# Macaron layer on one Trainium2 core: two first-key steps instead of one beside each unit of the last down-projection

## The chip, the cores and the metric

The kernel runs on one core of one Trainium2 chip. The metric is the device time of one execution in microseconds (us). All data are 32-bit floats. The engines are PE (matrix multiplication), DVE (vector), ACT (scalar functions), POOL (general) and SP, whose queue here issues most of the transfers.

## What is computed

The input x has 4 batches of 512 rows and 512 columns. The layer is a feed-forward part, an attention part and the same feed-forward part again:

```
x = x + 0.5 * ffn(layernorm(x))
x = x + attention(layernorm(x))
x = x + 0.5 * ffn(layernorm(x))

ffn(h):       gate, up, down = weights interpolated from a few control points (Catmull-Rom spline)
              return (silu(h @ gate.T) * (h @ up.T)) @ down.T          # 512 -> 2048 -> 512
attention(h): q, k, v, z from h @ W_qkvz; beta, g from h @ W_ba
              q, k, v = silu(conv of 4 taps along the rows)             # 16 key heads, 32 value heads
              q, k = rms_norm(q), rms_norm(k), each used by 2 value heads
              for each row t: S = S * exp(g_t)
                              S = S + k_t (x) ((v_t - k_t S) * beta_t)  # delta rule
                              o_t = q_t S
              return (rms_norm(o) * norm_w * silu(z)) @ W_out
```

## The kernel before

The first feed-forward part (`ffn`) goes batch by batch. A turn for batch b+1 computes gate and up products on PE, silu on ACT and the product of both on DVE, and stores the hidden values to memory; POOL then gathers them back in the order in which the spline's structure repeats (`gather`). The down-projection of a batch (`project`, a nested function of `ffn`) has 32 "units": 4 `sums` (the pm matmuls, line 482), 16 `blocks` (y, L492, 3 or 4 groups of 32 rows in 4 PSUM banks), 4 `rest` (L495) and 8 `total` (L498). ACT then moves each of the four y tiles to yg, and four more units, `back(g)`, transpose yg into y_pt (L509, in the PSUM banks of y) and add y_pt to the residual ffn_xr piece by piece on DVE (L537). After the last of them SP stores the batch (L515). The four `back` units of a batch are run at the start of the next turn, or, for the last batch, at the very end (`plan["tail"]`).

The attention works through 64 pairs of batch and key head, in "slots". Ahead of slot 0 stand its first steps, a generator (`attention`) that the feed-forward part drives through the argument `beside`: each `next` emits one step. There are 90: 13 for the layernorm of batch 0 and its transposition, then 77 for the first eight keys, seven for each key number `un`, overlapped over three key numbers. In the first four steps of a key one matmul of its projection pj is emitted (L1041; w_k is its weight, loaded by L1091). A step or more later follow the four taps of the convolution (ACT acc L1049, three DVE acc L1051), the silu (ACT th L1059, DVE k L1063), and with the seventh step two keys later the key's small blocks (PE pkk L1072, ACT ksq L1112, mean square on DVE L1077 to L1080, POOL rsk L1082, weights L1124 to L1130, POOL wed L1134, the scan L1141 and dd L1144). With the seventh step of key 2 come the gate sums `sums` (pgs L1012, pe L1021), whose result goes through memory: decay_c and decay_b (L1027, with a POOL memset L1025 ahead of each) and back as ad (L1103). Each step also lets the inverse of the first four keys' triangular blocks (`invert`, DVE L1155 to L1174) advance twice, once it has been made, which is with the seventh step of key 6. The last three DVE instructions of the first steps are memsets of tt and nn (L1695), and the generator then yields None. Slot 0 begins with pj of w_q and w_v and the block pqq (L1072, of q).

During these first steps PSUM has one bank for all products of the attention (pj, pgs, pe), since the four y banks and the two of pm hold the rest, and w_k has one buffer. The order on PE, DVE, ACT and POOL is the order in which the program emits (`by_hand`); each engine executes in that order. A scheduler orders SP in this part. `later(n, f)` puts f into a calendar that `tick` works off, n ticks on; the first steps have a calendar of their own with their own ticks. In `run`, each round emits one gather step, one unit and one first step.

The last part of `ffn` in the kernel before is then: a run over the 16 units left from batch 2 with a first step each; the four `back` units of batch 2 with a first step each; 14 first steps alone; 32 units of batch 3 with a first step each; the four `back` units of batch 3 with a first step each; then the 20 first steps that are left.

Of the kernel before, what the change touches and what calls it, by code (L numbers as in the profile page):

```python
# [23 lines left out]
NT = S // P  # L24
# [240 lines left out]
def tile_macaron(ctx, tc, x, w_qkvz, w_ba, conv_w, dt_bias, a_log, norm_w, w_out, cps, consts, grid, starts, out):  # L265
    nc = tc.nc
    B = x.shape[0]
# [31 lines left out]
    def ffn(src, dst, build, beside=iter(())):  # L299
        with ExitStack() as st:  # L300
# [21 lines left out]
            def tick():  # L322
                clock[0] += 1
                for f in calendar.pop(clock[0], ()):
                    f()

            def drain():
                while calendar:
                    tick()

            def load(b, name, pool):
                xt = pool.tile([P, NT, H], F32, name=name)
                nc.sync.dma_start(xt, src(b).rearrange("(t p) h -> p t h", p=P))
                return xt
# [14 lines left out]
            def features(xt):  # L349

                xnT = io.tile([P, NC, S], F32, name="ffn_xnT")
                ft = [fp.tile([P, S], F32, name="ft") for _ in range(NG_F)]
                xn, stat = {}, {}

                def stats():
                    stat["mv"], stat["rstd"] = statistics(xt)

                def norm(t):
                    mv, rstd = stat["mv"], stat["rstd"]
                    xn[t] = wk.tile([P, H], F32, name="ln_xn", bufs=3)  # L360
                    nc.vector.tensor_scalar(
                        xn[t], xt[:, t, :], mv[:, t, 0:1], rstd[:, t : t + 1], ALU.subtract, ALU.mult
                    )

                def turn(t):
                    pt = ps.tile([P, NC, P], F32, name="ln_pt", tag="tp")
                    for c in range(NC):
                        nc.tensor.transpose(pt[:, c, :], xn[t][:, c * P : (c + 1) * P], ident)
                    later(1, lambda: nc.scalar.copy(xnT[:, :, t * P : (t + 1) * P], pt))

                def interpolate(g):
                    pf = ps.tile([P, S], F32, name="pf", tag="tp")
                    for c in range(NC):
                        nc.tensor.matmul(
                            pf[NODES * c : NODES * (c + 1)], lag[:, c, NODES * g : NODES * (g + 1)], xnT[:, c, :],
                            start=True, stop=True,
                        )
                    later(1, lambda: nc.scalar.copy(ft[g], pf))

                turns = [lambda t=t: turn(t) for t in range(NT)]  # L380
                inter = [lambda g=g: interpolate(g) for g in range(NG_F)]
                return ft, stats, [lambda t=t: norm(t) for t in range(NT)], turns, inter
# [44 lines left out]
            def hidden(b, ft):  # L427

                to, box = hid[b % 2], {}

                def gate(k):
                    if build and b == 0:
                        block(k, wr, we, cm)
                    product(k, 0)

                def product(k, m):
                    at = (k % 2) * P
                    pm = box[m] = gu.tile([P, S], F32, name=("pg", "pu")[m], tag="gu")
                    nc.tensor.matmul(pm, wc[k // 2][:, m, at : at + P], ft[k // 2], start=True, stop=True)  # L439
                    if m:  # L440
                        pg = box[0]
                        later(1, lambda: finish(k, pg, pm))

                def finish(k, pg, pu):
                    sg = wk.tile([P, S], F32, name="ffn_sg")
                    nc.scalar.activation(sg, pg, AF.Silu)
                    it = wk.tile([P, S], F32, name="ffn_it", bufs=4)
                    nc.vector.tensor_tensor(it, pu, sg, ALU.mult)  # L448
                    nc.sync.dma_start(to[k * P : (k + 1) * P, :], it)

                return [f for k in range(NB) for f in (lambda k=k: gate(k), lambda k=k: product(k, 1))]

            def gather(b):
                to, nat = hid[b % 2], []

                def step(v):
                    nt = np_.tile([P, S], F32, name="nat")
                    nc.gpsimd.indirect_dma_start(  # L458
                        out=nt, out_offset=None, in_=to[:, :],
                        in_offset=bass.IndirectOffsetOnAxis(ap=idx[:, v : v + 1], axis=0),  # L460
                    )
                    nat.append(nt)

                return nat, [lambda v=v: step(v) for v in range(NB)]
# [82 lines left out]
            plan = {"nxt": None, "tail": [], "ft": ft}  # L547

            def turn_of(b):


                main = hidden(b + 1, plan["ft"]) if b + 1 < B else []
                norms, turns, inter = [], [], []
                if plan["nxt"]:
                    plan["ft"], _, norms, turns, inter = plan["nxt"]
                    plan["nxt"] = None
                units, back = [], []
                if b >= 0:
                    units, back = project(b, plan["nat"])
                plan["nat"], steps = gather(b + 1)  # L560
                tail, early_ = plan["tail"], []
                for i in range(4):
                    early_ += [*tail[i : i + 1], *turns[i : i + 1]]
                early_ += inter
                lead = 6 * 2 if b >= 0 else len(main)
                for i, f in enumerate(main):
                    if b + 3 < B:
                        if i == 16:
                            xt = load(b + 3, "ffn_x", io)
                        if i == 28:  # L570
                            plan["nxt"] = features(xt)
                            plan["nxt"][1]()
                    for n_ in norms[i : i + 1]:
                        n_()
                    f()
                    tick()
                    n = -(-len(early_) // max(1, lead - i)) if i < lead else 0
                    if i >= 2 or not turns:
                        for f in early_[:n]:
                            f()  # L580
                            tick()
                        early_ = early_[n:]
                    if i >= lead:
                        keep = 16 if b + 2 == B else 0
                        n = -(-(len(units) - keep) // (len(main) - i))
                        for f in units[:n]:
                            f()
                            tick()
                        units = units[n:]
                drain()  # L590
                plan["tail"] = back
                return early_ + units, steps if b + 1 < B else []

            def run(units, steps, beside=iter(())):
                while units or steps:
                    for f in steps[:1]:
                        f()
                    for f in units[:1]:
                        f()
                        tick()  # L600
                    next(beside, None)
                    units, steps = units[1:], steps[1:]

            by_hand = lambda *more: tc.manual_schedule(
# [6 lines left out]
            if build:  # L611
                first = hidden(0, plan["ft"])
                ft, _, norms, turns, inter = plan["nxt"] or (None, None, [], [], [])
# [16 lines left out]
            with by_hand(nc.sync):  # L630
                left = [], []
                if build:
                    plan["nat"], steps = gather(0)
                    left = [], steps
                for b in range(0 if build else -1, B - 1):
                    run(*left)
                    left = turn_of(b)

            early.close()
            with by_hand():  # L640
                also = beside if B > 2 else iter(())
                run(*left, also)
                units, _ = turn_of(B - 1)
                run(units[:NT], [], also)

                for _ in range(14):
                    next(also, None)
                run(units[NT:], [], also)
                run(plan["tail"], [], also)
                drain()  # L650
                for step in beside:
                    if step is None:
                        break

    def spline_weights(st, scratch, wc, ps):

# [1053 lines left out]

    steps = attention()
    ffn(lambda b: x[b], lambda b: x1[b], True, steps)
    for _ in steps:
        pass
    ffn(lambda b: x2[b], lambda b: out[b], False)


# [30 lines left out]
```

## Time and profile before

| what | value |
|---|---|
| time, median of 3 runs | 3822.8 us (3818.41, 3822.8, 3823.15) |
| profiled execution, its own time | 3876.63 us |
| span of the profiled execution | 3874.8 us |
| mean granted PE clock in it | 0.966 |
| PE, DVE, ACT, POOL busy, share of the span | 93%, 68%, 38%, 22% |
| batch 2's last units and batch 0's layernorm, then the 14 steps alone | to 392 us, then to 410 us |
| 32 units of batch 3 and its y_pt | 410 to 467 us |
| rest of the first steps | to 514 us |

The profile is one execution on the chip. Its times are microseconds from the start of the span. A timeline row gives the start, the length, the engine, the line of the kernel, the operation, its output and inputs, the shape, how many instructions are merged and, in brackets, how long the engine was idle before it and which instruction ended the wait. One fp32 product of PE appears as more than one matmul record, so a pj step of one contraction block is a row "x2". A row of the window table gives the busy time of each engine in one stretch, the granted PE clock as a share of full speed, the busy share of the DMA engines and what they moved.

### The profile page before, as it was taken

The numbers are of one execution on the slowest core, as the hardware profiler recorded it, in microseconds if no ns is written. First come the engines' busy times: TensorE is split into PE (matmuls) and PEld (weight loads), VectorE is DVE, ScalarE is ACT, GpSimd is POOL, SyncE is SP. The second block draws the span as 40 slices with busy tenths as digits, with TensorE's granted clock in tenths as the row PEclk, the third lists the DMA queues.
The fourth block names the chain that finished last, engine by engine and source line by source line (L and its number), as shares of the span: only waits on it lengthen the run. The fifth ranks groups of instructions, "written<-read, shape, count | busy, mean of one in ns | idle before, by whom it ended". The sixth has DMA issues, their size and how long they took to land.

```text
span 3874.8 us, 62477 instructions
## 1 busy us (share of the span) xinstructions
PE 3587.5 (93%) x24568; PEld 1969.3 (51%) x24568; DVE 2633.2 (68%) x5928; ACT 1464.5 (38%) x3440; POOL 852.4 (22%) x655
## 2 busy tenths in 40 slices
PE   5988779999999999999999999999999999988798
PEld 2333345555555555555555555555555555553233
DVE  5223687878878788788878887877888777643221
ACT  2322124444444444444444444444444434433121
POOL 2113112222222222222222222222222222211211
PEclk8999889999999999999999999999999999989998
DMA  4435321222222222122112221221222111104442
GB/s 140 150 117 187 88 66 47 62 63 61 59 65 70 80 64 71 51 63 61 58 58 80 66 62 57 64 73 58 60 84 60 54 61 58 55 12 157 148 144 87
DMA packets 303094, 302.25 MB, mean 78 GB/s; under 512 B 96881, under 2 KB 231313, under 8 KB 302225
## 3 DMA queue, kind: packets, MB, share of 16 engines
q1 hardware_dynamic: 292560, 264.70, 22.0%
q0 software_dynamic: 10240, 33.56, 2.8%
q8 instruction: 194, 3.18, 0.3%
q14 instruction: 100, 0.81, 0.1%
HBM read 247.60 MB, written 50.59 MB: 77 GB/s over the span
## 4 chain that ended last, share of the span: by engine, by line
PE 44%; DVE 36%; ACT 8%; POOL 5%; issue 3%; another core or an unknown queue 1%; DMA 1%; SPq 0%; DVEq 0%; ACTq 0%; POOLq 0%
DVE acc L1051 12%; PE py L1507 7%; PE pz L1359 6%; DVE vT L1063 4%; PE pj L1041 4%; PE pg L439 3%; PE pu L439 3%; PE y L492 3%; POOL oo L1480 3%; DVE ee L1227 3%; PE pks L1398 2%; POOL orr L1479 2%; ACT tq L1415 2%; PE pu L1344 2%; ACT oo L1485 2%
## 5 line engine op out<-in xcount | busy, mean ns | idle before, releaser
L1051 DVE SCALAR_TENSOR_TENSOR acc<-pj,cw,acc 128x511 f32<-128x511 f32 (+2 forms) x768 | 573.5, 747 | 160.1 <-ACT acc L1049 141.2
L1041 PE MATMUL pj<-xnT,w_v 128*128 128x512 f32 x1024 | 521.0, 602 | 0.0
L1507 PE MATMUL py<-w_o,gT 128*128 128x512 f32 x1024 | 514.9, 616 | 0.4
L1359 PE MATMUL pz<-w_z,xnT 128*128 128x512 f32 x1024 | 514.5, 614 | 0.0
L448 DVE TENSOR_TENSOR ffn_it<-pu,ffn_sg 128x512 f32<-128x512 f32 x128 | 88.4, 691 | 406.4 <-PE pu L439 231.6
L1041 PE MATMUL pj<-xnT,w_q 128*128 128x512 f32 x512 | 255.9, 603 | 9.4 <-ACT ksq L1112 9.4
L1041 PE MATMUL pj<-xnT,w_k 128*128 128x512 f32 x512 | 254.7, 599 | 3.9 <-DVE acc L1051 3.2
L1415 ACT ACTIVATE tq<-pks,rqe 128x128 f32<-128x128 f32 x384 | 120.4, 364 | 339.7 <-DVE rq L1256 195.9
L1059 ACT ACTIVATE th<-acc 128x512 f32<-128x512 f32 x256 | 163.0, 637 | 216.9 <-DVE acc L1051 215.3
L1485 ACT ACTIVATE oo<-oo,orr 128x128 f32<-128x128 f32 x512 | 162.6, 389 | 205.9 <-POOL oo L1480 205.9
L1049 ACT ACTIVATE acc<-pj,cw 128x512 f32<-128x512 f32 x256 | 175.3, 685 | 160.4 <-PE pj L1041 159.1
L1507 PEld LDWEIGHTS py<-w_o,gT 128*128 128x128 f32 x1024 | 171.6, 192 | 106.4 <-issue 95.3
L1359 PEld LDWEIGHTS pz<-w_z,xnT 128*128 128x128 f32 x1024 | 169.7, 190 | 99.5 <-issue 88.5
L1082 POOL TENSOR_TENSOR rsq<-msq,phalf 128x4 f32<-128x4 f32 x64 | 64.9, 1014 | 681.6 <-DVE msq L1080 681.6
L1082 POOL TENSOR_TENSOR rsk<-msk,phalf 128x4 f32<-128x4 f32 x64 | 66.9, 1045 | 664.5 <-DVE msk L1080 657.4
L1041 PEld LDWEIGHTS pj<-xnT,w_v 128*128 128x128 f32 x1024 | 170.6, 191 | 70.8 <-issue 64.1
L1241 POOL TENSOR_TENSOR ks<-kn,ws 128x1024 f32<-128x1024 f32 x64 | 121.8, 1902 | 378.2 <-DVE ws L1234 358.9
L1063 DVE SCALAR_TENSOR_TENSOR vT<-th,acc 128x512 f32<-128x512 f32 x128 | 184.8, 1444 | 23.1 <-ACT th L1059 23.1
L458 POOL DMA_INDIRECT nat<-hid,idx x128 | 122.9, 960 | 337.0 <-PE y_pt L509 134.2
L1473 DVE TENSOR_REDUCE om<-osq 128x4 f32<-128x512 f32 x128 | 87.1, 681 | 139.6 <-ACT osq L1472 139.6
L1166 DVE TENSOR_TENSOR inv<-inv,inv_tmp 128x30 f32<-128x30 f32 (+14 forms) x480 | 169.0, 352 | 16.5
L1423 PEld LDWEIGHTS pzz<-rr,tt 128*128 128x128 f32 x768 | 114.9, 193 | 113.1 <-issue 54.7
(213 smaller groups left out, 6874.5 us busy)
## 6 DMA issues: line engine op xcount, KB each, us to landing
hid<-ffn_it SPq DMA_DIRECT2D x128, 256.0 KB
w_v<-in_L_attn_W_qkvz SPq DMA_DIRECT2D x64, 512.0 KB
w_z<-in_L_attn_W_qkvz SPq DMA_DIRECT2D x64, 512.0 KB
ab<-decay_c SPq DMA_DIRECT2D x64, 512.0 KB
w_o<-in_L_attn_W_out SPq DMA_DIRECT2D x32, 1024.0 KB
w_k<-in_L_attn_W_qkvz SPq DMA_DIRECT2D x64, 256.0 KB
w_q<-in_L_attn_W_qkvz SPq DMA_DIRECT2D x64, 256.0 KB
ad<-decay_b SPq DMA_DIRECT2D x256, 32.0 KB
```

Of the source, the lines that this page charges most:

```text
L439: nc.tensor.matmul(pm, wc[k // 2][:, m, at : at + P], ft[k // 2], start=True, stop=True)
L1041: nc.tensor.matmul(pj, w()[:, c, col : col + DK], xnT[:, c, :], start=c == 0, stop=c == NC - 1)
L1049: nc.scalar.activation(acc, pj, AF.Copy, scale=cw[:, ch, 3:4])
L1051: nc.vector.scalar_tensor_tensor(acc[:, d:], pj[:, : S - d], cw[:, ch, 3 - d : 4 - d], acc[:, d:], ALU.mult, ALU.add)
L1059: nc.scalar.activation(th, box["acc"], AF.Tanh)
L1063: nc.vector.scalar_tensor_tensor(dest(), box["th"], 1.0, box["acc"], ALU.add, ALU.mult)
L1082: nc.gpsimd.tensor_tensor(rs, ms, phalf[:, :NT], ALU.pow)
L1166: nc.vector.tensor_tensor(ee[:, j + 1 :, :j], ee[:, j + 1 :, :j], tj, ALU.add)
L1359: nc.tensor.matmul(pz, xnT[:, c, t * P : (t + 1) * P], pair["wz"][:, c].rearrange("p j k -> p (j k)"), start=c == 0, stop=c == NC - 1,)
L1415: nc.scalar.activation(tq[:, r], pks[:, 1, r], AF.Copy, scale=s["rqe"][:, t, r : r + 1])
L1485: nc.scalar.activation(s["oo"][:, t, r], s["oo"][:, t, r], AF.Copy, scale=s["orr"][:, u : u + 1])
L1507: nc.tensor.matmul(box["py"], pair["gT"][r][:, t, :], pair["wo"][:, r, :], start=r == 0, stop=r == 3)
```

## The change

`run` gets a number `pace`: how many first steps follow each unit. For the turn of batch 3 (its four `back` units of batch 2 and 32 units of down-projection, in one run now) and for the four `back` units of batch 3 it is two instead of one. The 14 steps alone are dropped. With 16 steps beside batch 2's units, 72 beside the 36 units and two more, all 90 steps are emitted by the first two `back` units of batch 3, so none are left for the end. The generator is wrapped so that it stops at its None; what follows None stays behind the feed-forward part, as before. Each step and unit emits what it emitted before.

```diff
-            def run(units, steps, beside=iter(())):
+            def run(units, steps, beside=iter(()), pace=1):
                 while units or steps:
                     for f in steps[:1]:
                         f()
                     for f in units[:1]:
                         f()
                         tick()
-                    next(beside, None)
+                    for _ in range(pace):
+                        next(beside, None)
                     units, steps = units[1:], steps[1:]
...
             with by_hand():
-                also = beside if B > 2 else iter(())
+                first_steps = iter(beside.__next__, None)
+                also = first_steps if B > 2 else iter(())
                 run(*left, also)
-                units, _ = turn_of(B - 1)
-                run(units[:NT], [], also)
-
-                for _ in range(14):
-                    next(also, None)
-                run(units[NT:], [], also)
-                run(plan["tail"], [], also)
+                run(*turn_of(B - 1), also, 2)
+                run(plan["tail"], [], also, 2)
                 drain()
-                for step in beside:
-                    if step is None:
-                        break
+                for _ in first_steps:
+                    pass
```

On PE the order between pj of key 1 and the first pgs and pm changes, then pj and y alternate in another proportion. On DVE the last additions of ffn_xr (batch 3) come after the work of the last keys, with the memsets among them, instead of in the middle of the inversion. On SP the store of batch 2 is issued earlier, the store of batch 3 later, and the loads of w_k, ad, ab and w_o change their places. On POOL ee (L1221) moves behind one more rsk.

## The prediction

> **What bounds the kernel now.** I read the page first, for who is busy over the whole run, then the table of 10 us windows, to see which engine bounds the stretch that the change touches, then the timelines of PE, DVE and the DMA queue (SP) there.
>
> The page's first part: PE is busy nearly always, so the end moves only by what PE idles.
>
> ```profile
> PE 3587.5 (93%) x24568; PEld 1969.3 (51%) x24568; DVE 2633.2 (68%) x5928; ACT 1464.5 (38%) x3440; POOL 852.4 (22%) x655
> ```
>
> Windows (length, then busy us of PE, PEld, DVE, ACT, POOL, then PE's clock, DMA share, GB/s):
>
> ```profile
> 400.00:410.00 10.00, 5.47 (x18) 2.61 (x18) 5.18 (x12) 2.22 (x5) 0.00 (x0) 0.96 0.09 26
> 430.00:440.00 10.00, 10.00 (x94) 3.48 (x94) 5.09 (x13) 1.48 (x3) 1.93 (x2) 1.00 0.18 41
> 470.00:480.00 10.00, 0.00 (x0) 0.00 (x0) 9.72 (x31) 0.90 (x2) 0.00 (x0) 0.53 0.44 129
> 490.00:500.00 10.00, 3.81 (x5) 1.73 (x6) 9.21 (x31) 0.27 (x1) 1.40 (x2) 0.50 0.20 55
> 530.00:540.00 10.00, 10.00 (x113) 5.15 (x111) 7.33 (x18) 5.14 (x11) 4.08 (x2) 1.00 0.10 29
> ```
>
> Three stages. To 410 PE has holes: the 14 steps alone. From 410 to 467 PE is full and DVE half idle. From 467 to 520 DVE is full and PE stands: DVE sets that end, and whatever PE saves ahead of it counts only if DVE's stretch starts sooner. From 520 on PE is full again, so a shift at 520 reaches the end of the kernel.
>
> PE's timeline (start, length, line, operation, what it waited for):
>
> ```profile
> 392.37 5.21 PE L1041 MATMUL pj<-xnT,w_k 128*128 128x512 f32 x8
> 400.76 3.67 PE L1041 MATMUL pj<-xnT,w_k 128*128 128x512 f32 x8 [3.18 <-DVE acc L1051]
> 407.62 0.68 PE L1012 MATMUL pgs<-g,cst 128*128 128x128 f32 x4 [3.18 <-issue]
> 424.59 1.10 PE L1041 MATMUL pj<-xnT,w_k 128*128 128x512 f32 x2 [0.71 <-ACT fm L484]
> 436.24 1.12 PE L1041 MATMUL pj<-xnT,w_k 128*128 128x512 f32 x2
> 486.10 0.66 PE L1072 MATMUL pkk<-k 128*32 128x32 f32 x32 [19.21 <-DVE k L1063]
> 496.19 6.22 PE L1041 MATMUL pj<-xnT,w_q 128*128 128x512 f32 x8 [9.44 <-ACT ksq L1112]
> 502.25 4.45 PE L1041 MATMUL pj<-xnT,w_v 128*128 128x512 f32 x10
> 519.39 0.66 PE L1072 MATMUL pqq<-q 128*32 128x32 f32 x32 [12.69 <-DVE q L1063]
> 519.98 3.78 PE L1041 MATMUL pj<-xnT,w_v 128*128 128x512 f32 x4
> ```
>
> DVE's timeline: the inversion starts at 458.95, and from there DVE works without a break to the last memset.
>
> ```profile
> 454.94 2.32 DVE L1051 SCALAR_TENSOR_TENSOR acc<-pj,cw,acc 128x511 f32<-128x511 f32 x3 [4.20 <-ACT acc L1049]
> 458.95 1.94 DVE L1155 STREAM_TRANSPOSE inv<-dd 128x1024 f32<-128x1024 f32 x1
> 485.87 1.50 DVE L537 TENSOR_TENSOR ffn_xr<-y_pt,ffn_xr 128x4 f32<-128x4 f32 x16
> 513.52 0.48 DVE L1695 MEMSET nn<- 64x512 f32 x1
> ```
>
> SP's timeline: fourth key's load, and the store of the last batch.
>
> ```profile
> 421.47 0.40 SPq L1091 DMA_DIRECT2D w_k<-in_L_attn_W_qkvz x1
> 487.40 0.36 SPq L515 DMA_DIRECT2D x<-ffn_xr x1
> ```
>
> The load lands in time for the matmul at 424.59, 3.1 us after its issue.
>
> **The change part by part.** No instruction is added or dropped; the order changes between 375 and 525 us. All is set against the profiled execution (3876.63 us, 54 above the median 3822.8; the difference is carried over).
>
> *1. The 14 steps alone go.* They took 392.4 to 410.5, with 6.9 us of PE holes (3.18, 3.18, 0.58). Now they stand between the four transpositions of batch 2 and the first sums and blocks. That hides the holes but delays the chain. Key 1's last matmul comes at 398.2 behind two more y_pt groups, its taps on DVE behind more ffn_xr additions, so key 2 starts at 402.9 (was 400.8). The first y matmuls need the banks of y_pt1 to y_pt3, free after the last ffn_xr of batch 2 at about 406.7, and key 2's last matmul is queued behind them: 411, so pgs at 414.2 (was 407.6). On SP and POOL follow decay_c, the memset, decay_b, eight ad issues (4.71 us) and key 4's w_k: 13.9 us from pgs before, some 0.9 less now, since the store of batch 2 is issued ahead of them. w_k at 427.1, its matmul at 430.2 instead of 424.59: **+5.6**.
>
> *2. Two steps a unit.* A key has 7 steps, four with a matmul of 1.07 us. Before: 7 units of 1.07 and 4 of 1.07 are 11.7 us, the distance of 424.59 and 436.24. Now 3.5 units: 8.1 us of PE work. But next key's first matmul needs the only bank, free 3.05 us after the last matmul (ACT acc 0.69, three DVE acc 2.32), and the only w_k buffer, 3.1 us from issue to use. Before, 4 units (4.3 us) covered that; now two and a pkk cover 2.0, so PE waits 1.1: 9.2 us a key. Two keys and key 6's own matmuls gain 5.3 of the 5.6. The inversion starts at 459.2: **+0.3**. PE's saved holes thus end at a DVE that starts no sooner.
>
> A rule bears on the 3.1 us. The Trainium skill, "DMA: Bandwidth & Descriptors", section "Anatomy of one DMA — SWDGE (gpsimd) path", puts a transfer at 2.0 us and its bytes at 436 GB/s: an estimate of 2.6 for these 256 KB, on a path that isn't this queue. It would make the key 8.7 and the sum 1.3 lower. I take the trace's 3.1.
>
> *3. DVE's stretch.* From 458.95 to 514.00 are 55.05 us. The operations stay, the last additions of ffn_xr (0.84+1.25+1.50+1.66+1.50 = 6.75 us) move to its end. Of the small waits (0.79, 1.19, 0.79 on POOL) the scan ee now covers one: **−0.8**. So it ends at T = 513.5.
>
> *4. What has lost its cover.* In before w_q and five w_v matmuls ran at 496 to 507 in DVE's shadow. Now w_q's first matmul takes the bank of y_pt3, whose last ffn_xr addition is DVE's last work before T. So w_q (6.06 us), ACT's copy (0.69), then taps q to pqq (515.62 to 519.39, 3.77) follow T: pqq at T+10.8 instead of T+5.4: **+5.4**. PE is warm then, so the w_v group behind it, 3.78 at a clock of 0.58 to 0.74, takes 2.0 with what surrounds it: **−1.6**.
>
> A rule speaks here: the skill's "TensorE: Matmul & The Clock Gate", section "What's actually happening", has PE at half clock after an idle window of about 3.4 us, and full after 3.4 us of work. By it w_q would be cold for 3.4 and then twice as fast, 4.8 us, the sum 1.3 lower. The row has clock 0.50 and 6.06 us for all four contraction steps, after holes as long as those expected here: I take 6.06.
>
> *5. Moved at no cost.* SP: the last x store is issued at T, and q's silu and pqq wait for its landing; before it landed after some 5.6 us (as the store at 415.2 did), needed at T+10: 4 us of slack. ab, w_q, w_v, w_z wait for the last FFN matmul (480.3, as it is queued behind key 7's pkk, which waits for DVE's k at 477.5): ab at 487.4, needed at 495.6. w_o moves behind ad: not used for long. POOL: ee stands behind one more rsk (1.0), with the same slack. ACT: yg2 and yg3 behind ksq at 486.5, needed at 503. If such a cover is gone, DVE or pqq waits for the excess, 1:1.
>
> Sum: 0.3 − 0.8 + 5.4 − 1.6 = **+3.3 us**, 0.09%. About 0.2% (7.6 us) is what a measurement of this kernel can tell from no change, so this is no change: 3826, its own range 3821 to 3832, for the front's +5.6 (2 to 8) and w_q's 4.8 to 6.1.
>
> **The rivals.** *Slower: the keys keep no 9.2 us.* Place: 425 to 455, where DVE has its taps in order with the rest. Each key has some 5 us of DVE work (5.09 in an 11.7 us key's window) and ACT's part; if taps find an addition, a th or a mean square ahead of them, bank and next key are late, and y behind the matmul too. Price: 1.5 to 3 us a key, three keys, 4.5 to 9 ahead of the inversion, passed on whole: 3831 to 3835. It decides from 10.6 us a key (3 × 1.4 = 4.3, with 3.3 over 7.6). For: DVE's in-order queue, one bank, one buffer. Against: DVE idles 4.20 ahead of a tap at 454.94. More of the same kind (a front later than 430) reaches 3841.
>
> *Faster: the gain stays.* Keys at 8.1 us (the load hidden) and a front late by 2 instead of 5.6 start the inversion at 452.3, 6.9 sooner; if w_q also isn't held (the bank free before DVE's end), 5.4 less its 1.6 go too, and if DVE's two small waits left on POOL (1.19 and 0.79) are covered as the third is, 2.0 more: 3.3 − 6.9 − 3.8 − 2.0 = −9.4, or 3813. For: 6.9 us of holes do vanish. Against: the 3.18 waits in the trace on exactly this bank; a gain needs two steps wrong together.
>
> *It doesn't do what it says:* the order on all engines does move, so only a shift that cancels is left; it is in the first case.
>
> **How the numbers follow.** Forecast 0.55 (0.40 within 0.2%, 0.15 above by the upper ends of its terms); slower rival 0.29; faster rival 0.16 (0.14 past −0.2%, 0.02 within). Slower 0.44, same 0.42, faster 0.14. Range 3813 to 3839 leaves out some 0.1 below and 0.1 above.
>
> **What would show it.** Right: pgs near 414, key 4 near 430, keys 9.2 apart with holes of 1 us, inversion near 459, w_q after the last ffn_xr near 513.5, pqq near 524. Wrong: inversion before 455 or w_q ahead of DVE's end (faster); keys over 10.6 apart, or pqq waiting for the x store (slower).

## The result: slower by 0.3%, and the profile after

| | kernel before | changed kernel |
|---|---|---|
| time, median of 8 runs | 3824.48 us (3818.41 to 3827.38) | 3835.24 us (3833.35 to 3838.28) |
| ratio to before | | 1.0029, 95% interval 1.0019 to 1.0038 |
| span of the profiled execution | 3874.8 us | 3831.9 us |

The change costs 10.8 us (by the interval 7 to 15). The forecast case, 3826, is 9 us too low, and the time lies above its own range (3821 to 3832); the whole range, 3813 to 3839, holds it by the part given to the slower rival.

The span of before is from an execution that is long elsewhere: from the last output projection of the attention (the last start of py, 3503.0 there and 3492.5 in the changed kernel) to the end it took 372 us, the changed kernel's 339. So the two traces are not laid over each other from the start of the span but from the end of pb, the gate projection ahead of key 1: 391.49 in before (384.82 + 6.67), 372.05 in the changed kernel. pb starts 9.0 us after the first matmul of key 0 in both (375.80 and 357.38), so up to there the change shifted nothing. All times below called "from pb" are so counted. In before pb itself took 1.03 us longer; a second trace of before (e5) bounds what this does to the comparison.

PE's timeline of the changed kernel, from pb to slot 0 (columns as in the prediction):

```profile
366.41 5.64 PE L948 MATMUL pb<-wba,xnT 128*128 128x64 f32 x32 [2.74 <-issue]
383.25 1.10 PE L1037 MATMUL pj<-xnT,w_k 128*128 128x512 f32 x2 [3.43 <-DVE acc L1047]
386.01 2.92 PE L492 MATMUL y<-nat,wr 32*128 32x512 f32 x4 [0.38 <-DVE ffn_xr L537]
388.86 3.46 PE L1037 MATMUL pj<-xnT,w_k 128*128 128x512 f32 x4
397.55 0.68 PE L1008 MATMUL pgs<-g,cst 128*128 128x128 f32 x4 [2.11 <-issue]
414.54 2.04 PE L1037 MATMUL pj<-xnT,w_k 128*128 128x512 f32 x2 [4.73 <-DVE w L1124]
416.51 2.09 PE L492 MATMUL y<-nat,wr 32*128 32x512 f32 x8
426.13 1.96 PE L1037 MATMUL pj<-xnT,w_k 128*128 128x512 f32 x4 [0.65 <-DVE acc L1047]
435.25 1.10 PE L1037 MATMUL pj<-xnT,w_k 128*128 128x512 f32 x2 [1.87 <-DVE dd L1140]
436.28 2.09 PE L492 MATMUL y<-nat,wr 32*128 32x512 f32 x8
446.24 1.96 PE L1037 MATMUL pj<-xnT,w_k 128*128 128x512 f32 x4 [0.65 <-DVE acc L1047]
502.68 6.27 PE L1037 MATMUL pj<-xnT,w_q 128*128 128x512 f32 x8 [23.55 <-issue]
513.58 0.46 PE L1068 MATMUL pqq<-q 128*32 128x32 f32 x32 [0.34 <-DVE q L1059]
513.97 1.98 PE L1037 MATMUL pj<-xnT,w_v 128*128 128x512 f32 x4
```

Keys 4 to 7 start at 414.54, 426.13, 435.25 and 446.24: 11.6, 9.1 and 11.0 us apart, where 9.2 was predicted. The long distances are those that begin with a long hole (4.73 and 1.87 us), and after these holes PE is slow: the same eight y matmuls that take 1.14 us elsewhere take 2.09. The window table says that this is the clock (PEclk, third number from the end):

```profile
380.00:390.00 10.00, 6.38 (x12) 2.21 (x13) 6.47 (x29) 1.59 (x4) 0.00 (x0) 0.75 0.25 90
...
410.00:420.00 10.00, 5.46 (x13) 1.90 (x14) 3.38 (x11) 0.79 (x2) 1.99 (x2) 0.66 0.25 50
420.00:430.00 10.00, 9.35 (x74) 3.06 (x73) 5.10 (x13) 1.58 (x3) 1.31 (x1) 1.00 0.17 39
430.00:440.00 10.00, 8.13 (x64) 3.00 (x63) 5.09 (x13) 1.58 (x3) 2.54 (x3) 0.83 0.18 41
```

Narrower windows of the same table place the changes. The granted clock is 0.50 ("cold" below; "warm" is 1.00) from 385.04 to 391.87, 398.70 to 402.11, 412.35 to 419.18 and 436.24 to 439.66. These stretches are one or two times 3.41 us long, and they start 4, 4 and 7 times 3.41 us apart: the clock changes on a fixed grid, and it does so in all ten traces. In the step of the grid ahead of the last fall, 432.83 to 436.24, PE was busy for 45%, since the hole of 1.87 us lies wholly in it.

The wait of 4.73 us is put down to a DVE operation (w, L1124) that ended at 414.50. That is a coincidence: in e1 below, with the same order on PE and DVE, this matmul starts 3.4 us before that operation. SP's timeline has the true releaser. The load of key 4's weight stands behind eight ad issues, is issued at 411.42, 3.1 us ahead of the matmul, and lands 3.0 us later.

```profile
406.54 4.78 SPq L1099 DMA_DIRECT2D ad<-decay_b  x8
411.42 0.40 SPq L1087 DMA_DIRECT2D w_k<-in_L_attn_W_qkvz  x1
502.61 0.38 SPq L515 DMA_DIRECT2D x<-ffn_xr  x1
```

Key 6's weight, not held up by ad, is issued at 431.10 and lands only after 4.0 us (keys 5 and 7: 2.8), just ahead of the matmul at 435.25. That is the hole of 1.87 us; why this load was slow is open.

DVE's timeline, the inversion's start, the taps of a key, and the two ends of its stretch:

```profile
443.82 2.31 DVE L1047 SCALAR_TENSOR_TENSOR acc<-pj,cw,acc 128x511 f32<-128x511 f32 x3 [5.77 <-ACT acc L1045]
447.83 1.93 DVE L1151 STREAM_TRANSPOSE inv<-dd 128x1024 f32<-128x1024 f32 x1
498.18 4.40 DVE L537 TENSOR_TENSOR ffn_xr<-y_pt,ffn_xr 128x12 f32<-128x12 f32 x35
502.49 1.91 DVE L1151 STREAM_TRANSPOSE inv<-dd 128x1024 f32<-128x1024 f32 x1
```

The inversion starts 75.8 us from pb (before: 67.5), the stretch ends, where the next transposition starts, at 130.4 (122.4), pqq starts at 141.5 (127.9), and the third matmul step of key 8, well inside slot 0, at 148.5 (137.7). These are 8.3, 8.0, 13.6 and 10.9 us more. The last one is the measured cost: from there the shift stays at 9 to 11 us to the end of the attention.

### The profile page after: what moved, and what is told of

Its sections match the earlier page's. It is cut to its first block, busy times and chain, and to the rows that moved or that the text cites. A ratio compares the mean times of both kernels' runs of the same rounds, so it can differ in the third digit from the quotient of the medians.

```text
span 3831.9 us, 62480 instructions
## 1 busy us (share of the span) xinstructions
PE 3582.2 (93%) x24568; PEld 1965.4 (51%) x24568; DVE 2632.5 (69%) x5928; ACT 1463.6 (38%) x3440; POOL 851.6 (22%) x655
## 4 chain that ended last, share of the span: by engine, by line
PE 43%; DVE 35%; ACT 8%; POOL 6%; issue 4%; DMA 3%; SPq 1%; DVEq 0%; POOLq 0%; ACTq 0%
DVE acc L1047 13%; PE py L1503 7%; PE pz L1355 6%; DVE vT L1059 4%; PE pj L1037 4%; POOL oo L1476 3%; PE y L492 3%; PE pg L439 3%; DVE ee L1223 3%; PE pu L439 3%; PE pks L1394 2%; POOL orr L1475 2%; ACT tq L1411 2%; PE pu L1340 2%; ACT th L1055 2%
```

## The experiments

Each was timed beside the kernel before. That took 3823.8 us beside e1 to e4 and 3880.1 us beside e5 to e8, so ratios are compared, not times. "us" beside a ratio is the ratio's distance from 1 times the time of before.

**e1: two buffers for w_k.**

```diff
-s["w_k"] = w1.tile([P, NC, DK], F32, name="w_k")
+s["w_k"] = w1.tile([P, NC, DK], F32, name="w_k",
+                   tag="rt" if pa is None and n % 2 else "w_k")
```

> The changed kernel, with two buffers for w_k in the first steps (odd keys load into rt's, which is free until the inversion ends), so that a key's weight is loaded one key ahead. Order on PE, DVE, ACT and POOL as in the changed kernel. Clock theory (the holes of 4.73 us before key 4 and 1.87 us before key 6 wait for w_k, and PE then works at half clock, which costs 3.0 and 1.9 us more): both holes shrink to about 0.7 us, PE stays at full clock, keys are 9.1 us apart, the inversion starts about 10 us sooner, the time is about 3825 us. Holes without a clock effect: 4.0 + 1.2 us sooner, about 3830. Rival of the prediction (DVE's queue makes the keys late): nothing, 3835.

Measured: 3825.41 us, ratio 1.0007 (0.9999 to 1.0016), +2.7 us against before, 8 us under the changed kernel. PE's timeline:

```profile
407.31 1.10 PE L1037 MATMUL pj<-xnT,w_k 128*128 128x512 f32 x2 [0.72 <-ACT ksq L1108]
416.70 1.95 PE L1037 MATMUL pj<-xnT,w_k 128*128 128x512 f32 x4 [0.65 <-issue]
424.81 1.10 PE L1037 MATMUL pj<-xnT,w_k 128*128 128x512 f32 x2 [0.86 <-ACT ksq L1108]
434.20 1.96 PE L1037 MATMUL pj<-xnT,w_k 128*128 128x512 f32 x4 [0.66 <-issue]
```

The time is the one expected. Both long holes are gone, keys 4 to 7 are 9.4, 8.1 and 9.4 us apart, all at full speed, and the inversion starts 68.5 us from pb, 7.3 sooner than in the changed kernel. It is not the 10 expected, in part because PE was still cold at key 3: two of its steps (397.78) took 3.37 us, in the changed kernel 1.98 (402.39). Holes of 0.7 to 0.9 us stay, of the one bank. With holes and clock effect gone together, this alone doesn't separate the two.

**e2: the holes filled with work.**

```diff
...
+for _ in range({4: 5, 6: 2}.get(un, 0)):     # ahead of key 4's and key 6's first step
+    nc.tensor.matmul(made[un - 3]["s"]["kk"][:, P:], ident,
+                     batches[0]["xnT"][:, 0, P:], start=True, stop=True)
```

> The changed kernel with work added: five matmuls of 128x384 into an unused part of pkk's bank ahead of key 4's first matmul, two ahead of key 6's, in the holes in which PE waits for w_k. Their results are not read. Clock theory: key 4 and key 6 run at full clock, 3.0 + 1.9 us less: about 3830 us, although PE has some 5 us more to do. Rivals (DVE's queue, or the holes alone): no gain, 3835 or up to 1 us more.

Measured: 3832.47 us, ratio 1.0024 (1.0015 to 1.0033), +9.2 us, where 3830 us had been expected; the intervals of this and of the changed kernel overlap. In the trace the gain is plain. PE's timeline (L1676 is the added work):

```profile
412.13 3.49 PE L1676 MATMUL pkk<-xnT,ident 128*128 128x384 f32 x10 [0.40 <-ACT ksq L1112]
415.46 1.02 PE L1037 MATMUL pj<-xnT,w_k 128*128 128x512 f32 x2
432.43 1.56 PE L1676 MATMUL pkk<-xnT,ident 128*128 128x384 f32 x4 [0.40 <-ACT ksq L1112]
433.82 1.02 PE L1037 MATMUL pj<-xnT,w_k 128*128 128x512 f32 x2
443.13 1.95 PE L1037 MATMUL pj<-xnT,w_k 128*128 128x512 f32 x4 [0.65 <-DVE acc L1047]
```

Two rows of its window table, at full clock where the changed kernel had 0.66 and 0.83:

```profile
410.00:420.00 10.00, 9.61 (x76) 4.16 (x72) 5.09 (x13) 1.49 (x4) 2.00 (x2) 1.00 0.27 53
430.00:440.00 10.00, 9.61 (x80) 3.53 (x74) 5.09 (x13) 1.34 (x4) 1.93 (x2) 1.00 0.18 39
```

Key 4 starts no sooner (43.0 us from pb, 42.5 in the changed kernel), yet key 7 starts at 70.7 instead of 74.2 and the inversion at 72.3 instead of 75.8: 3.5 us won by more work, with DVE's order untouched. The keys are 9.3, 9.1 and 9.3 us apart, as predicted. In this execution that is the clock; the time's interval is too wide to show 3.5 us by itself.

**e3: the 14 steps alone put back, two steps a unit kept behind them.**

```diff
-run(*turn_of(B - 1), also, 2)
+units, _ = turn_of(B - 1)
+run(units[:NT], [], also)
+for _ in range(14):
+    next(also, None)
+run(units[NT:], [], also, 2)
```

> The 14 first steps alone are put back, with one step beside each of the four back units of batch 2, as before; two steps beside each of the 32 units of batch 3 and its tail, as in the change. If the late front is the larger part (key 4 at +9.4 us against before): key 4 starts as before, the inversion about 1 us sooner than before (33.3 us from key 4 to it, as in the changed kernel), the end costs +2.9: about 3826 us. If the two steps a unit are what costs: near 3835.

Measured: 3820.47 us, ratio 0.9995 (0.9987 to 1.0003): not slower than before, 13 us under the changed kernel, where 3826 had been expected. PE's timeline:

```profile
402.97 1.12 PE L1041 MATMUL pj<-xnT,w_k 128*128 128x512 f32 x2
412.38 1.95 PE L1041 MATMUL pj<-xnT,w_k 128*128 128x512 f32 x4 [0.82 <-DVE acc L1051]
420.50 1.10 PE L1041 MATMUL pj<-xnT,w_k 128*128 128x512 f32 x2 [0.86 <-DVE acc L1051]
429.88 1.95 PE L1041 MATMUL pj<-xnT,w_k 128*128 128x512 f32 x4 [0.65 <-DVE acc L1051]
```

Key 4 starts 31.8 us from pb (before: 33.1), and there is no hole ahead of it, against my expectation. The reason is on SP: here the scheduler put the store of batch 2 late and key 4's w_k ahead of the eight ad issues (9.8 us after pgs instead of 13.9). From key 4 to the inversion are 28.5 us, and the inversion starts at 60.3, 7.1 us sooner than before. So two steps a unit do gain, where PE stays at full clock. The trace gives 7 us at key 8's third step and 4.7 to 6.5 at the last pqq of the attention (by the two traces of before), the times 1.9 (a loss of 1 to a gain of 5); where the rest goes is open.

**e4: one step a unit from the inversion on.**

```diff
-run(*turn_of(B - 1), also, 2)
-run(plan["tail"], [], also, 2)
+units, _ = turn_of(B - 1)
+run(units[:23], [], also, 2)
+run(units[23:], [], also)
+run(plan["tail"], [], also)
```

> The changed kernel until the inversion's first operation (23 units at two steps), then one first step for each remaining unit and for the tail, the rest of the steps alone. So the last additions to ffn_xr come in the middle of DVE's stretch again and w_q runs in its shadow. Theory of the end (w_q behind the last addition costs 5.6 us, a warm PE behind it gives 2.7 back): 3832 us, the inversion's start unchanged. If w_q's place doesn't matter: 3835.

Measured: 3826.85 us, ratio 1.0008 (1.0001 to 1.0014), 8 us under the changed kernel, where 3 had been expected. PE's timeline:

```profile
413.18 2.04 PE L1039 MATMUL pj<-xnT,w_k 128*128 128x512 f32 x2 [4.69 <-DMA w_k<-in_L_attn_W_qkvz]
434.05 1.10 PE L1039 MATMUL pj<-xnT,w_k 128*128 128x512 f32 x2 [1.56 <-ACT th L1057]
436.15 1.98 PE L1039 MATMUL pj<-xnT,w_k 128*128 128x512 f32 x4
490.54 5.32 PE L1039 MATMUL pj<-xnT,w_q 128*128 128x512 f32 x8 [24.72 <-issue]
504.11 0.65 PE L1070 MATMUL pqq<-q 128*32 128x32 f32 x32 [3.96 <-DVE q L1061]
```

The first row names the transfer as what key 4 waits for. w_q runs at 490 to 496, ahead of the end of DVE's stretch at 498.59, and pqq follows that end by 5.5 us (changed kernel 11.1, before 5.5). The v matmuls behind it are slow again, as in before: from pqq to key 8's third step 8.6 us (changed kernel 7.0). That is 4.0 of the 7.1 us by which this trace is shorter there. Another 2.0 stem from ahead of the inversion, where this execution kept the full clock over key 6's hole of 1.56 us (the changed kernel lost it over 1.87), and 1.1 from a shorter DVE stretch.

**e5: the kernel before again.** No edit.

> The kernel before once more, for a second trace of it: in the first one the 32 pb matmuls took 6.67 us against 5.64 in all later traces, and the last feed-forward part was some 30 us longer than in the changed kernel's trace. All theories: no difference between the two in what matters here, the inversion starts 67.5 us (or 1 us more, if pb was 1 us too long) after the end of pb, pqq 60.4 us after that.

Measured: 3881.63 us, where before has a median of 3880.12 on that chip. From pb: key 4 at 34.3, the inversion at 68.6, pqq at 128.9, key 8's third step at 137.4; the first trace has 33.1, 67.5, 127.9 and 137.7. Two traces of one kernel differ here by about 1 us, so differences of 3 us and more can be read.

**e6 and e7: the best of both.** e6 is e3 with one step a unit from the inversion on; e7 has six units without a step between.

```diff
 run(units[:NT], [], also)
 for _ in range(14):
     next(also, None)
-run(units[NT:], [], also, 2)
-run(plan["tail"], [], also, 2)
+run(units[NT : NT + 14], [], also, 2)
+run(units[NT + 14 : NT + 20], [])            # e7 only; e6 has none of this line
+run(units[NT + 20 :], [], also)              # e6: from NT + 14
+run(plan["tail"], [], also)
```

> The 14 steps alone put back as in e3, two steps beside the first 14 units of batch 3 (to the inversion), then one step beside each of the other 18 and the tail, the last six steps alone. The inversion starts as in e3, 7 us sooner than before. If w_q comes free of DVE's last work again: pqq 5.5 us after DVE's stretch (e3: 8.4) but with a cold PE behind it, in sum about 1 us better than e3: 3 to 8 us under the kernel before. If the last additions still stand at the end of DVE's stretch, as e3.

> As e6, but six units without a step right after the inversion's first operation, so that the last additions come earlier in DVE's stretch and w_q starts well before its end. Key 7 is 6 us later on PE, beside the inversion's operations on DVE, which take about as long: the same end of DVE's stretch, w_q in its shadow, 4 to 8 us under the kernel before. If key 7's taps are then missed by DVE, up to 5 us worse than e6.

Measured: e6 0.9966 (0.9952 to 0.9979), 13 us under the kernel before (3 to 8 expected) and the best version, from five runs; e7 0.9991 (0.9982 to 0.9999), 3.5 us under it (4 to 8 expected). e6 on DVE, then on PE:

```profile
458.80 1.95 DVE L1156 STREAM_TRANSPOSE inv<-dd 128x1024 f32<-128x1024 f32 x1
511.50 1.80 DVE L1156 STREAM_TRANSPOSE inv<-dd 128x1024 f32<-128x1024 f32 x1
```

```profile
506.66 6.37 PE L1042 MATMUL pj<-xnT,w_q 128*128 128x512 f32 x8 [26.06 <-DVE rk L1127]
517.65 0.46 PE L1073 MATMUL pqq<-q 128*32 128x32 f32 x32 [0.33 <-DVE q L1064]
```

pb ends at 399.02 here: the inversion starts at 59.8, as in e3, and DVE's stretch is 52.7 us long instead of 55, ending at 112.5. w_q is under way 4.8 us ahead of that end, so pqq comes 6.2 after it, with a warm PE behind. By the trace e6 gains 12 us at key 8's third step, which agrees with its time. In e7 the six units moved key 7's projection back, and the stretch grew to 57.0 us. That is 4.3 of the 8.3 us by which e7's trace is longer there than e6's; 2.5 stem from ahead of the inversion, where key 2 ran cold (5.37 us for 3.67), and the rest from a cold PE behind pqq.

**e8: one step beside the four back units.**

```diff
-run(*turn_of(B - 1), also, 2)
+units, _ = turn_of(B - 1)
+run(units[:NT], [], also)
+run(units[NT:], [], also, 2)
```

> The changed kernel with one step instead of two beside the four back units of batch 2, still without the 14 steps alone. Tells apart which part of the front delays key 4: the steps of key 1 between the transpositions and additions of batch 2 (then y's banks come free earlier here, key 4 is at about +4 us instead of +9.4, the time 4 to 6 us under the changed kernel, about 3829 us), or the units between the steps of keys 1 and 2 (then key 4 stays at +8 to +10 and the time near 3835).

Measured: ratio 1.0019 (1.0012 to 1.0026), +7.4 us; by the trace 4 at key 8's third step. PE's timeline:

```profile
402.37 1.09 PE L492 MATMUL y<-nat,wr 32*128 32x512 f32 x2 [2.23 <-DVE ffn_xr L537]
413.80 0.68 PE L1010 MATMUL pgs<-g,cst 128*128 128x128 f32 x4 [2.10 <-issue]
429.97 2.05 PE L1039 MATMUL pj<-xnT,w_k 128*128 128x512 f32 x2 [4.17 <-DMA w_k<-in_L_attn_W_qkvz]
```

From pb (391.25): pgs at 22.6, between the changed kernel's 25.5 and before's 16.1 to 17.6; key 4 at 38.7, between 42.5 and 33.1 to 34.3. So both answers hold in part: some 3 to 4 us come from the steps among the back units, some 5 from the units between the steps of keys 1 and 2. The hole of 4.17 us and the cold start behind it are as in the changed kernel, since w_k is behind the ad issues here too.

## Where the prediction held and where it failed, step by step

The range held the time, the forecast case did not: no change was forecast, and 10.8 us came. That the range was wide enough is in part luck. The slower rival made room for 4.5 to 9 us in the keys by a cause on DVE; a loss of about that size, 4.2 us, came in the keys, but from the clock.

| step | predicted | first traces of both kernels |
|---|---|---|
| 1. front: key 4 | +5.6 | +9.4 |
| 2. key 4 to the inversion (29.0 against 34.4 us) | −5.3 | −1.1 |
| 3. DVE's stretch | −0.8 | −0.3 |
| 4. w_q uncovered | +5.4 | +5.6 |
| 4. warm PE behind it | −1.6 | −2.7 |
| sum | +3.3 | +10.9 |

Against the second trace of before (e5) a row differs by up to 1.2 us, and the sum is +11.1.

*Step 1 had the mechanism and missed the size.* Key 2 starts at 11.2 us from pb, the 402.9 of the prediction's frame to within 0.2, and y's first block waits for the last ffn_xr, as said. But PE was cold from 385.04 to 391.87 (0.75 in the row 380 to 390 above): y and pj there take 2.92 and 3.46 us (the latter 1.98 when warm), so pgs was 9.4 late and not 6.6. The 0.9 us credited for the earlier store of batch 2 was no gain either: from pgs to w_k's issue are 13.9 us in both kernels, and ad starts 1.5 us behind decay_b in both, whether the store stands between them or not.

*Step 2 is the step that failed.* Its arithmetic is right where PE keeps its clock: 29.0 us from key 4 to the inversion were predicted, e1 has 28.5, e2 29.3, e3 28.5. The changed kernel has 33.3. The sum counted the holes but not what a hole does to the work behind it: from key 4 on PE was cold for 4.64 us behind the first hole and 3.41 behind the second, and half of that, 4.0 us, is nearly all of the 4.3 missing. I had weighed the clock rule of the Trainium skill ("TensorE: Matmul & The Clock Gate") at w_q alone, where a cold PE was seen in before; the same page's section "HAM oscillation — how this bites in real kernels" describes a case like this, short bursts of matmuls behind waits for a load that cross the window of about 3.4 us, each burst starting cold. The 4.73 us hole agrees with it; that the clock also fell after 1.87 us goes beyond what that section says. And step 1 put key 4's start at the landing of its weight without asking how long PE would stand ahead of it: 4.73 us.

*Steps 3 and 4* came out within 1.1 us: pqq follows DVE's end by 11.1 us (predicted 10.8, though the terms listed add up to 10.5), and e4 shows that it is w_q's place, not the work. w_q was as cold as the row of before had it: it took 6.27 us, not the 4.8 that I had estimated from the page, since the clock stayed at half for its first 5.25 us. *Step 5*: the store at 502.61 held up nothing: pqq waited 0.34 us.

*The rivals.* The slower one had place and size: 4.2 us in the keys, which are 10.6 apart on average, the point from which it was to decide. Its mechanism was wrong: DVE stood idle ahead of the taps (5.77 us in the row above), and e2 wins the time back without a change on DVE. The faster one failed on key 4; its first half, a gain at the inversion, came true in e3 and e6, where the front is the old one. Its keys at 8.1 us, and the 8.7 under the rule on loads, left out that the bank binds as well: e1 hides the load and has 9.0 on average.

*Shown and argued.* That key 4's load behind the ad issues makes the hole is shown by e1 and the waits of e4 and e8; that the clock and not DVE costs the 3.5 us behind the holes by e2's trace and the clock's own record. The split of the front is from e8's trace alone. The times put e3 nearer to before than its trace does, and that stays open.

## What to carry to other kernels

A hole on PE costs more than its length when it lets the clock fall: before work is packed closer around a load, look for the queue position of that load, not only for its duration. Filling a stretch that looks idle (the 14 steps alone) is no gain if those steps are the head of the chain that sets the end; keep the head of the chain short, and put the denser mixing behind it, as e6 does. And when an addition moves to the end of the bounding engine, check which bank it holds and who is next in it.

## What the runs showed of the hardware

The clock of PE changed on a grid of 3.41 us, in all ten traces. What counted was how busy PE was in the step before, not the length of one hole. Of the steps at full clock between 300 and 3700 us, all 110 in which PE was busy for less than 40% were followed by a cold one, and all but 4 of more than 9000 with over 60% by a warm one; between 40% and 60% it went both ways (50 cold, 65 warm). Out of the cold it came only behind a step that was 80% busy or more. So a hole of 1.87 us let the clock fall in the changed kernel (45% busy in its step), and one of 1.56 us in e4 did not (54%).

After over 20 us without a matmul PE took 5.3 to 6.7 us for w_q's four steps (eight traces), against 3.67 us for key 2's in before: the clock stayed at half for the first 3.3 to 6.1 us of them. Added matmuls (5.1 us of them, e2) made the trace 3.5 us shorter up to key 8's third step.
